# A two-layer convolution block: work moved between ScalarE, VectorE and GpSimd, two transfers reshaped, PSUM banks from a table and a new order of issue

## The chip, the core and the metric

The kernel runs on one core of one Trainium2 chip. A core has TensorE (PE in the profile; its weight loads are listed as PEld), VectorE (DVE), ScalarE (ACT), GpSimd (POOL) and SyncE (SP), each with its own queue of instructions that it works off in order; SP's queue here issues nearly all DMAs. The engines meet at semaphores. SBUF is the on-chip working memory with 128 partitions; PSUM holds eight banks of 128 x 512 floats, into which TensorE writes. The metric is device time in microseconds of the whole launch, lower is better. All data are 32-bit floats.

## What is computed

Input: 16 images of 256 channels, 64 x 64 pixels. Two layers follow one another; the helper names are those of the reference, and what doesn't matter here is cut.

```python
x = x + attention(_gn(x), g_norm, w_qkv, w_out, b_out, g_out)       # layer 0
x = x + experts(_gn(x), router_w, router_b, dw_w, dw_b, pw_w, pw_b)  # layer 1

def attention(x, ...):                    # linear attention, 4 heads of 32
    xn = rmsnorm(x, g_norm)               # over channels, per pixel
    q, k, v = split(einsum('oc,bchw->bohw', w_qkv, xn))
    q = softmax(q, axis=-2); k = softmax(k, axis=-1)
    context = einsum('bhdn,bhen->bhde', k, v)
    out = einsum('bhde,bhdn->bhen', context, q * scale)
    out = einsum('oc,bchw->bohw', w_out, out) + b_out
    return rmsnorm(out, g_out)            # the "output norm"

def experts(x, ...):                      # 2 of 4 experts per image
    w = renormalised top-2 of softmax(mean(x) @ router_w.T + router_b)
    return sum(w[e] * (pw_w[e] @ gelu(depthwise3x3(x, dw_w[e]) + dw_b[e]) + pw_b[e]))
```

`_gn` is a group norm with 32 groups over an image. The experts of an image cannot begin before its router has chosen, and the router needs the mean of the whole image after layer 0.

## The kernel before

A test at the start takes the fast branch, `pipelined_path`; the other branch, `general_path`, does not run here. In the fast branch every step of every image is a small Python function (`norm`, `turn_x`, `out_norm`, `tap1`, ...). A row for each is entered in a list with a phase ("in", "q", "out", "route", "c", "v", "x"), an image number b and a group, quarter or half. A table of numbers, `PLAN` (lines 60 to 819, some 3100 entries), gives each row a place in time; `place` adds the image's start, the group's slot and the step's own entry, or an override for one image and group (`"tap18@e2.3"`: second image from the end, quarter 3). The rows are sorted by place and issued in that order, so the order of each engine's queue is the order of that list. Nothing rearranges it afterwards. An image's period is 64 units of the plan. Three phases of three images overlap: while TensorE and VectorE work on the experts of image b, layer 0 of image b+1 and the statistics of b+2 run between.

Layer 0 works in 8 groups of 512 pixels (`NG`, `GT`). For a group: `load_b` fetches the two halves of 128 channels, `norm` (L1019) applies the group norm; images 0 and 1 (`EARLY`) do it on VectorE, the others on ScalarE, in 224 instructions of 128 x 512. TensorE transposes to pixels (`turn_x`), ScalarE squares and sums, GpSimd makes the reciprocal root (`token_scale`, through `rsqrt`, L956), TensorE projects q and k (`project`), ScalarE takes the exponent (`evacuate`), `context` accumulates. GpSimd divides q by its sums in place (`q_norm`). Once the image's context is mixed with the output weights, `attend` (L1155) makes the output of 256 pixels into a bank `po`; ScalarE squares it (`out_squares`), GpSimd makes the scale s (`out_scale`), and `out_norm` (L1176) multiplies `po` by s into the tile `ob`. In images 0, 1 and 15 ScalarE does that, as two instructions of 128 x 256; in the 13 others VectorE, as one of 128 x 512. `out_turn` (L1185) transposes `ob` back on TensorE, `out_add` (L1193) adds it to the image on VectorE. Reading `po` in `out_norm` is what frees that bank.

The router's chain (`gn1_sums` to `pick_taps`, L1210 to L1283) is a run of small instructions, nearly all of them on VectorE; `expert_index` gives SyncE the number of the expert for `fetch`, and `lace` puts the fetched weights in place on GpSimd.

Layer 1 treats its channels in two ways. The first 128 (functions with a 0) run on TensorE as a banded product: `pad0` writes the padded image into SBUF, `lay` stores it in HBM, `spread` (L1384) reads it back as patches, 54 rows of 1054 floats for each half r of the partitions and each t of eight; four patch buffers `xr` rotate. `conv0` multiplies, `gelu0` evacuates, `put` writes the result to HBM, and `take` (L1454) reads it back by channel into `hp`, 32 rows of 16 KB per transfer. The last 128 (functions with a 1) run as sums on VectorE: `start1` (L1464) opens the sum of an expert on ScalarE with the first tap and the bias, `tap1` (L1472) adds the eight others on VectorE, and `gelu1` follows on ScalarE. `pointwise` (L1484) multiplies both by the experts' weights, and `residual` adds them to the image, from where `store` writes it out.

PSUM: one bank holds the context; the other seven are one rotating pool. `bank` (L971) takes the next of them, so a new tile waits for whoever read the tile seven before it.

Of the kernel before, what the change touches and what calls it, by code (L numbers as in the profile page):

```python
# [24 lines left out]
NE = 4  # L25
# [24 lines left out]
NU = P // (2 * CB)  # L50
NXR = 4
# [9 lines left out]
    "load_x1": 2.02, "mean": 1.19, "means": 13.36, "dev": 13.73, "devs": 17.34, "scale": 17.85,  # L61
    "bias": 21.91, "in_lead": 26.39, "norm0": -8.96, "norm1": -3.87, "turn_x0": 0.72, "x_sq0": 1.77,
    "x_sq1": 2.31, "turn_x1": 1.43, "x_sq2": 3.45, "x_sq3": 3.25, "token": 4.42, "x_keep0": 5.53,
    "x_keep1": 5.77, "x_keep2": 5.97, "x_keep3": 6.03, "project0": 3.18, "evacuate0": 6.05,
    "project1": 3.64, "evacuate1": 6.46, "project2": 3.67, "evacuate2": 6.47, "project3": 4.06,
    "evacuate3": 6.58, "context": 9.48, "q_sum": 8.22, "q_norm": 11.06, "q_turn": 14.73,
    "q_keep": 16.31, "mix_a": 9.53, "mix_turn": 10.09, "mix_v": 11.08, "mix_vv": 11.63,
    "mix_b": 11.82, "mix_out": 13.35, "mix_c": 13.91, "mix_lead": 16.02, "attend0": -1.14,
    "out_sq0": -0.04, "out_sq1": 0.35, "out_scale0": 0.42, "out_norm0": 1.58, "attend1": -0.28,
    "out_sq2": 1.31, "out_sq3": 1.37, "out_scale1": 3.18, "out_norm1": 4.28, "out_turn0": 5.64,  # L70
    "out_add0": 6.51, "sq_sums0": 8.92, "out_turn1": 6.16, "out_add1": 7.06, "sq_sums1": 9.17,
    "sums1": 9.6, "means1": 9.77, "scale1": 10.52, "router": 10.97, "route": 11.89, "choose": 13.68,
    "pick_taps": 21.03, "route_lead": 21.97, "weigh": 29.78, "pick_bias": 41.15, "pad1": -10.35,
    "start0": -0.53, "tap01": 1.33, "tap02": 1.57, "tap03": 1.59, "tap04": 1.87, "tap05": 2.54,
    "tap06": 4.55, "tap07": 4.74, "tap08": 6.14, "gelu10": 13.51, "start1": 1.94, "tap11": 3.52,
    "tap12": 8.13, "tap13": 8.14, "tap14": 8.54, "tap15": 9.95, "tap16": 12.84, "tap17": 13.06,
    "tap18": 14.42, "gelu11": 15.46, "pw00": 16.32, "pw01": 16.45, "pw02": 17.78, "pw03": 17.83,
    "pw10": 16.09, "pw11": 16.24, "pw12": 19.85, "pw13": 20.43, "residual00": 19.8,
    "residual01": 20.37, "store0": 32.19, "residual10": 22.5, "residual11": 23.44, "store1": 26.19,
    "in_first": 0.96, "in_more": 1.71, "q_first": 3.46, "out_first": 27.07, "out_more": 37.75,  # L80
    "q_less": 0.19, "load_a0": -17.62, "load_a1": -6.91, "load_b0": -15.96, "load_b1": -6.67,
    "stats0": -13.55, "stats1": -1.94, "load_weights": 58, "scale_weights": -7.03,
    "end_pw00": 135.48, "end_pw01": -49.35, "end_pw02": 69.96, "end_pw03": 337.87,
    "end_residual00": 3.29, "end_residual01": 66.1, "end_pw10": 115.56, "end_pw11": -47.98,
    "end_pw12": -196, "end_pw13": -114.87, "end_residual10": -13.43, "end_residual11": 88.85,
    "x_0": 0.99, "x_1": -0.21, "x_2": -0.19, "x_e1": 5.09, "x_e2": 4, "route_0": -3.83,
    "route_1": 0.32, "route_2": -0.55, "route_e1": -1.2, "route_e2": -0.21, "out_0": -5.81,
    "out_1": -0.4, "out_2": 0.09, "out_e1": -1.85, "out_e2": -0.87, "q_0": -7.21, "q_1": -2.22,
    "q_2": 0.4, "q_e1": -1.65, "q_e2": -0.57, "in_0": -22.93, "in_1": 7.98, "in_2": 2.65,
    "in_e1": -1.58, "in_e2": 0.28, "pw04": -112.48, "pw14": -23.18, "x_last": 16.71,  # L90
    "v_last": 15.93, "v_e1": 3.4, "tap18@e2.3": 12.73, "start0@e1.3": -0.55, "x_sq2@2.2": 2.88,
    "gelu11@e1.2": 17.06, "tap03@0.1": 1.97, "project0@0.0": 2.01, "out_norm1@2.7": 4.71,
    "out_sq1@e2.0": 0.64, "out_scale1@1.2": 2.19, "evacuate0@1.2": 5.17, "context@1.7": 8.38,
    "out_scale1@0.0": 4.74, "q_norm@0.0": 15.63, "out_turn0@1.4": 5.23, "token@2.1": 4.75,
    "project0@2.7": 3.47, "context@0.7": 8.6, "attend1@e1.3": -2.08, "out_norm1@1.1": 3.87,
    "context@2.1": 7.79, "q_norm@0.6": 12.94, "out_norm0@1.1": 1.4, "gelu11@e2.3": 13.29,
    "evacuate2@1.7": 6.62, "out_norm1@0.6": 4.18, "evacuate2@2.2": 6.81, "project0@2.3": 4.02,
    "token@2.2": 4.19, "norm0@0.0": -14.16, "q_sum@0.0": 10.99, "x_sq2@2.6": 2.62,
    "norm1@0.0": -4.28, "out_norm1@e1.1": 5.78, "x_sq2@1.2": 2.18, "tap04@e2.2": 2.29,
    "x_keep0@0.5": 6.43, "out_turn0@1.2": 5.58, "evacuate3@1.7": 8.13, "x_sq2@2.5": 2.77,  # L100
    "turn_x0@0.0": -3.93, "out_scale0@1.2": 2.15, "tap13@2.0": 6.26, "x_keep3@1.2": 6.99,
    "out_turn0@1.3": 4.82, "q_sum@e2.6": 8.44, "x_sq2@0.0": -1.29, "scale1@0.0": 11.1,
    "token@0.1": 2.33, "q_sum@1.5": 10.67, "q_sum@1.1": 7.71, "tap12@e1.1": 3.08,
    "x_keep1@0.1": 3.76, "evacuate2@1.6": 5.71, "q_sum@1.3": 8.05, "route@0.0": 12.55,
    "x_sq2@1.4": 2.43, "q_turn@0.2": 15.05, "bias@0.7": 26.53, "token@1.4": 3.4,
    "pick_taps@e1.0": 23.22, "out_add0@2.5": 6.36, "means@0.7": 10.61, "dev@e2.7": 6.55,
    "evacuate3@1.2": 6.52, "x_sq3@1.4": 3.12, "x_keep1@0.7": 6.49, "mix_v@0.7": 11.95,
    "token@1.1": 4.49, "tap17@e2.3": 11.87, "out_turn0@e1.1": 7.3, "token@0.2": 4.15,
    "q_sum@1.2": 9.02, "out_norm0@1.2": 4.52, "x_keep0@0.7": 6.45, "mix_b@e1.7": 12.79,
    "choose@1.0": 14.4, "project0@e1.7": 2.76, "tap07@e1.2": 8.15, "tap11@e1.2": 5.96,  # L110
    "means@1.7": 3.31, "token@1.3": 3.93, "q_sum@e1.6": 8.87, "tap12@e2.0": 8.3,
    "out_scale0@1.3": 2.06, "route@e1.0": 12.62, "pick_taps@2.0": 19.25, "out_turn0@1.0": 5.21,
    "scale@0.7": 20.54, "tap06@e1.0": 3.75, "out_turn1@e2.2": 8.74, "token@0.7": 3.73,
    "q_sum@e2.7": 9.96, "stats0@e2.5": -12.47, "out_turn0@1.5": 5.79, "token@1.6": 3.52,
    "q_turn@e2.1": 14.09, "out_norm1@e2.5": 4.67, "weigh@0.0": 26.02, "x_sq2@1.0": 3.24,
    "out_turn0@0.3": 5.99, "turn_x0@2.2": -1.78, "mix_b@0.7": 18.63, "out_scale1@e2.6": 2.5,
    "gelu11@e1.0": 17.52, "token@e2.7": 4.04, "context@1.2": 12.21, "q_sum@e2.0": 7.26,
    "tap01@e1.3": 1.63, "tap12@e2.2": 6.87, "x_sq2@1.6": 3.27, "load_a1@1.6": -5.34,
# [704 lines left out]
def pipelined_path(ctx, tc, ring, st_0, wqkv, x, w_outT, b_out, g_out, router_wT, router_b, dw, dw_b, pwT, pw_b, out):  # L823
# [103 lines left out]
    def band_table():  # L927
# [5 lines left out]
        for dy in range(3):  # L933
            for dx in range(3):
# [5 lines left out]
                for u in range(QR, QR + dy):  # L940
                    k = 3 * QR + 2 * dx + u - QR
                    nc.gpsimd.tensor_copy(te[:, :, k * QR + u - dy : k * QR + u - dy + 1], w)
# [1343 lines left out]
```

## Time and profile before

| | us |
|---|---|
| runs of the kernel, median of 3 | 2681.89 |
| lowest and highest of them | 2674.61, 2682.42 |
| the profiled execution: time | 2665.43 |
| the profiled execution: span, first to last instruction | 2663.7 |
| granted clock of TensorE, mean | 0.97 |

The page of the profile gives for each engine how long it was busy, and cuts the span into 40 equal slices. In the first rows a digit is the busy share of a slice in tenths, in PEclk the clock granted to TensorE in tenths of full speed:

```profile
PE   6897999989899998989999898999989899997877
DVE  6565789879988898989988898988888888889887
ACT  3588988878788888878888887988888788875632
PEclk9998999999999999999999999999999999998999
DMA  4848788878778778777877887787877777866885
```

The middle of the run is even: one image follows another. The first three slices (the first image has nothing to overlap with) and the last four (the last image's experts) look different. A group of instructions is listed with its line, engine, operation, the tiles out<-in, count, busy time and mean; these are the groups that the change touches:

```profile
L1027 ACT ACTIVATE xg<-xb,bi,sc 128x512 f32<-128x512 f32 x224 | 182.6, 815 | 16.9 <-DMA xb<-in_x 14.4 <-PE pq L1066 2.3
L1467 ACT ACTIVATE acc<-pd,ds 128x1024 f32<-128x1024 f32 x128 | 158.9, 1242 | 21.5 <-PE pw L1503 11.7 <-POOL taps L1333 6.4 <-issue 1.7
L1183 DVE TENSOR_TENSOR ob<-po,s 128x512 f32<-128x512 f32 x208 | 141.3, 679 | 35.1 <-POOL s L960 33.6 <-PE tr L1188 1.2 <-POOL s L959 0.2
L1181 ACT ACTIVATE ob<-po,s 128x256 f32<-128x256 f32 x96 | 40.1, 479 | 14.6 <-POOL s L960 14.4
L1474 DVE SCALAR_TENSOR_TENSOR acc<-pd,ds,acc 128x1024 f32<-128x1024 f32 x1024 | 1324.0, 1298 | 44.7 <-ACT acc L1467 26.2 <-DMA xr<-lay 3.1
```

The time behind the second bar is the idle time of the engine just before those instructions, and what ended it.

### The profile page before, as it was taken

What the parts mean: (1) busy time and instruction counts of PE and PEld (TensorE: products, weight loads), DVE (VectorE), ACT (ScalarE), POOL (GpSimd) and SP (SyncE); (2) the same over time, 40 slices, a digit from 0 to 9 for tenths busy, and PEclk for the clock granted to TensorE, in tenths of its full rate; (3) what the DMA queues carried; (4) which work ended last, traced back from release to release, by engine and by line L of the source; (5) the groups of instructions that cost most, each with busy time, mean ns of one, the idle gap of its engine ahead of it and who ended that gap; (6) DMA issues with size and microseconds to landing.
All of it is one profiled execution on the core that took longest, in us unless ns stands there. A gap on an engine that the chain in (4) does not pass through costs nothing.

```text
span 2663.7 us, 50175 instructions
## 1 busy us (share of the span) xinstructions
PE 2404.0 (90%) x17204; PEld 1604.7 (60%) x17204; DVE 2244.2 (84%) x3489; ACT 2072.5 (78%) x4848; POOL 912.5 (34%) x1217
## 2 busy tenths in 40 slices
PE   6897999989899998989999898999989899997877
PEld 5675666656665665656666565666666566564433
DVE  6565789879988898989988898988888888889887
ACT  3588988878788888878888887988888788875632
POOL 4243343333333333334333243432333343433200
PEclk9998999999999999999999999999999999998999
DMA  4848788878778778777877887787877777866885
GB/s 145 103 127 224 227 230 233 232 226 242 221 226 238 227 236 247 228 227 228 232 228 240 240 240 222 230 235 228 247 216 222 222 206 209 232 186 197 227 226 176
DMA packets 410840, 581.15 MB, mean 218 GB/s; under 512 B 66000, under 2 KB 279504, under 8 KB 406480
## 3 DMA queue, kind: packets, MB, share of 16 engines
q1 hardware_dynamic: 377248, 575.36, 74.8%
q10 hardware_dynamic: 33328, 2.49, 1.6%
q8 instruction: 139, 2.28, 0.4%
q14 instruction: 125, 1.02, 0.1%
HBM read 402.49 MB, written 175.24 MB: 217 GB/s over the span
## 4 chain that ended last, share of the span: by engine, by line
PE 43%; DVE 21%; DMA 15%; ACT 8%; issue 6%; POOL 3%; SPq 3%; DVEq 0%; ACTq 0%; POOLq 0%
PE pw L1503 19%; DVE acc L1474 11%; PE pq L1066 7%; DMA hid<-hx 5%; PE pc L1084 4%; PE po L1160 4%; DMA hp<-hid 4%; PE dw L1432 3%; PE px L1035 2%; PE tr L1188 2%; DVE ring L1518 2%; DVE ob L1183 2%; DMA xr<-lay 2%; DVE ring L1197 2%; DMA lay<-pd 2%
## 5 line engine op out<-in xcount | busy, mean ns | idle before, releaser
L1474 DVE SCALAR_TENSOR_TENSOR acc<-pd,ds,acc 128x1024 f32<-128x1024 f32 x1024 | 1324.0, 1298 | 44.7 <-ACT acc L1467 26.2
L1503 PE MATMUL pw<-acc,ps 128*128 128x512 f32 x1024 | 496.5, 623 | 26.8 <-ACT acc L1482 24.4
L1066 PE MATMUL pq<-wqkv_n,xg 128*128 128x256 f32 x2048 | 487.5, 385 | 13.7 <-ACT e L1074 3.5
L1503 PE MATMUL pw<-hp,ps 128*128 128x512 f32 x1024 | 479.9, 604 | 18.4 <-DMA hp<-hid 15.5
L959 POOL TENSOR_SCALAR s<-ss 128x2 f32<-128x2 f32 x256 | 125.5, 490 | 1020.6 <-ACT junk L1168 1015.4
L1066 PEld LDWEIGHTS pq<-wqkv_n,xg 128*128 128x128 f32 x2048 | 383.1, 192 | 90.4 <-issue 19.1
L1503 PEld LDWEIGHTS pw<-acc,ps 128*128 128x128 f32 x1024 | 191.1, 199 | 229.9 <-issue 154.8
L1503 PEld LDWEIGHTS pw<-hp,ps 128*128 128x128 f32 x1024 | 189.2, 193 | 204.7 <-issue 196.5
L1042 ACT ACTIVATE jx<-px 128x256 f32<-128x256 f32 x512 | 196.3, 383 | 131.8 <-PE px L1035 122.4
L1160 PE MATMUL po<-mw,qt 128*128 128x256 f32 x1024 | 265.1, 389 | 9.9 <-DVE ring L1197 3.8
L1518 DVE SCALAR_TENSOR_TENSOR ring<-pw,bs,ring 128x512 f32<-128x512 f32 x248 | 180.8, 744 | 107.5 <-PE pw L1503 104.5
L1074 ACT ACTIVATE e<-pq,r 128x256 f32<-128x256 f32 x512 | 210.8, 477 | 58.8 <-PE pq L1066 45.0
L1197 DVE SCALAR_TENSOR_TENSOR ring<-tr,gout,ring 128x512 f32<-128x512 f32 x256 | 187.1, 746 | 81.2 <-PE tr L1188 75.9
L1084 PE MATMUL pc<-xt,e 128*128 128x257 f32 x1024 | 252.4, 389 | 2.5 <-ACT xt L1053 1.7
L960 POOL TENSOR_TENSOR s<-s,mhalf 128x2 f32<-128x2 f32 x256 | 243.7, 952 | 21.4
L1168 ACT ACTIVATE junk<-po 128x256 f32<-128x256 f32 x512 | 198.0, 387 | 60.9 <-PE po L1160 52.1
L1432 PE MATMUL dw<-xr,taps 55*32 55x128 f32 x8192 | 185.4, 283 | 61.7 <-DMA xr<-lay 30.0
L1188 PE MATMUL tr<-ident,ob 128*128 128x128 f32 x1024 | 162.1, 285 | 67.6 <-DVE ob L1183 46.4
L1160 PEld LDWEIGHTS po<-mw,qt 128*128 128x128 f32 x1024 | 186.0, 194 | 61.5 <-issue 22.0
L1432 PEld LDWEIGHTS dw<-xr,taps 55*32 55x32 f32 x8192 | 128.5, 108 | 147.0 <-issue 28.1
L1444 ACT ACTIVATE hx<-dw 128x512 f32<-128x512 f32 x256 | 148.4, 594 | 86.9 <-PE dw L1432 60.8
L1084 PEld LDWEIGHTS pc<-xt,e 128*128 128x128 f32 x1024 | 191.2, 195 | 33.2 <-issue 5.1
(146 smaller groups left out, 3533.4 us busy)
## 6 DMA issues: line engine op xcount, KB each, us to landing
xr<-lay SPq DMA_DIRECT2D x512, 197.6 KB
hid<-hx SPq DMA_DIRECT2D x256, 256.0 KB
hp<-hid SPq DMA_DIRECT2D x128, 512.0 KB
out<-ring SPq DMA_DIRECT2D x128, 512.0 KB
xa<-in_x SPq DMA_DIRECT2D x240, 256.0 KB
xb<-in_x SPq DMA_DIRECT2D x240, 256.0 KB
ring<-in_x SPq DMA_DIRECT2D x120, 512.0 KB
lay<-pd SPq DMA_DIRECT2D x32, 1188.0 KB
```

The source lines that it names most:

```text
L960: nc.gpsimd.tensor_tensor(out_t, out_t, mhalf[:, :n], ALU.pow)
L1066: nc.tensor.matmul(pq, xg[:, k, c * P : (c + 1) * P], wqkv[:, k, : 2 * HID], start=(k == 0), stop=(k == KH - 1),)
L1074: nc.scalar.activation(live["e", b, g][:, c], live["pq", b, g, c // 2][:, c % 2], AF.Exp, scale=live["r", b, g][:, c : c + 1],)
L1084: nc.tensor.matmul(live["pc", b], live["e", b, g][:, c, HID:], xt[g % 2][:, c], start=(g == 0 and c == 0), stop=(g == NG - 1 and c == CG - 1),
L1160: nc.tensor.matmul(po[:, c], qt[:, n * P : (n + 1) * P], live["mw", b], start=True, stop=True)
L1168: nc.scalar.activation(junk[:, :C], live["po", b, g, hf][:, c], AF.Square, accum_out=ss[:, c : c + 1])
L1188: nc.tensor.transpose(tr[:, c * P : (c + 1) * P], live["ob", b, g, c // 2][:, c % 2, k * P : (k + 1) * P], ident,)
L1197: nc.vector.scalar_tensor_tensor(xin, live.pop(("tr", b, g, k)), gout[:, k : k + 1], xin, ALU.mult, ALU.add, accum_out=live["sm", b][:, 0, ...
L1432: nc.tensor.matmul(pair[r][g * 2 * QR : (g + 1) * 2 * QR, s * HC : (s + 1) * HC], taps[ks, CB * t + i].rearrange("p i x -> p (i x)"), stri ...
L1474: nc.vector.scalar_tensor_tensor(acc, pd1[j % 2][:, t // 3 : t // 3 + QR, t % 3 : t % 3 + W], live["ds", b][:, i, t : t + 1], acc, ALU.mul ...
L1503: nc.tensor.matmul(po, w, rhs, start=begin, stop=end)
L1518: nc.vector.scalar_tensor_tensor(xo, po, bs, xo, ALU.add, ALU.add)
```

## The change

Six edits:

1. `norm` for images 2 to 15 goes from ScalarE to GpSimd, one tensor_scalar of 128 x 512 with two per-partition scalars each.
2. `start1` goes from ScalarE to GpSimd, one tensor_scalar of 128 x 1024 each.
3. `out_norm` of all images is two ScalarE instructions of 128 x 256; the VectorE form is gone.
4. `spread` reads the 54 rows of a half in one transfer instead of 48 and 6; the rows of the patch, and of the band table that it is multiplied with, are numbered 3u + dx throughout.
5. `take` reads 32 rows as four pieces of 4 KB each; the tile `hp` has four floats of padding behind each piece, so that pieces do not join, and `pointwise` indexes it accordingly.
6. `bank` takes a bank's number from a string, `BANKS`, one digit for each call, instead of rotating; `PLAN` has new numbers throughout (3121 entries), which sort the rows into a new order on every queue.

```diff
+HR = QR // 2 * HC
...
+BANKS = (
+    "012345601320463150361423640516352314306203502416502431414205206543125351025364351456320352"
...
+)
...
-        tb = work.tile([P, TOPK * QR * HC], FP, tag="hp", name="bands", bufs=1)
-        tb = tb[:, : NE * KP * QR]
+        tb = work.tile([P, 2 * TOPK, HR + 4], FP, tag="hp", name="bands", bufs=1)
+        tb = tb.rearrange("p s n -> p (s n)")[:, : NE * KP * QR]
...
-                    k = 3 * QR + 2 * dx + u - QR
+                    k = 3 * u + dx
...
+    turns = iter(BANKS)
...
     def bank(*key):
-        return banks.tile([P, 512], FP, tag="bank", name="_".join(map(str, key)))
+        tag = f"bank{next(turns)}"
+        return banks.tile([P, 512], FP, tag=tag, name="_".join(map(str, key)), bufs=1)
...
-            nc.scalar.activation(live["xg", b, g][:, k], xb, AF.Identity, bias=bi, scale=sc)
+            nc.gpsimd.tensor_scalar(live["xg", b, g][:, k], xb, sc, bi, ALU.mult, ALU.add)
...
         ob = new(work, [P, 2, C], "ob", b, g, hf, bufs=3)
         s, po = live.pop(("s", b, g, hf)), live.pop(("po", b, g, hf))
-        if b in (0, 1, NB - 1):
-            for c in range(2):
-                nc.scalar.activation(ob[:, c], po[:, c], AF.Copy, scale=s[:, c : c + 1])
-        else:
-            nc.vector.tensor_tensor(ob, po, s.unsqueeze(2).to_broadcast([P, 2, C]), ALU.mult)
+        for c in range(2):
+            nc.scalar.activation(ob[:, c], po[:, c], AF.Copy, scale=s[:, c : c + 1])
...
-            k0 = r * P // 2
-            (su, _), run1 = run.ap
+            rows, run1 = run.ap
             nc.sync.dma_start(
-                out=tile_t[k0 : k0 + 3 * QR, :n],
-                in_=bass.AP(run.tensor, run.offset, [[su, QR], [1, 3], run1]),
-            )
-            nc.sync.dma_start(
-                out=tile_t[k0 + 3 * QR : k0 + WK, :n],
-                in_=bass.AP(run.tensor, run.offset + QR * su, [[1, 3], [su, 2], run1]),
+                out=tile_t[r * P // 2 : r * P // 2 + WK, :n],
+                in_=bass.AP(run.tensor, run.offset, [rows, [1, 3], run1]),
             )
...
-            new(work, [P, TOPK * QR, HC], "hp", b, h, bufs=1)
+            new(work, [P, 2 * TOPK, HR + 4], "hp", b, h, bufs=1)
...
-            out=live["hp", b, h][cs].rearrange("c k x -> c (k x)"), in_=hids[h][cs]
+            out=live["hp", b, h][cs, :, :HR], in_=hids[h][cs].rearrange("c (s n) -> c s n", n=HR)
...
-        nc.scalar.activation(
-            acc, pd1[j % 2][:, 0:QR, 0:W], AF.Identity,
-            bias=ds[:, i, 9:10], scale=ds[:, i, 0:1],
+        nc.gpsimd.tensor_scalar(
+            acc, pd1[j % 2][:, 0:QR, 0:W], ds[:, i, 0:1], ds[:, i, 9:10], ALU.mult, ALU.add
         )
...
-                rhs = hp[:, i * QR + rows.start : i * QR + rows.stop, j % NB2 * W : (j % NB2 + 1) * W]
+                rhs = hp[:, 2 * i + q, :HR].rearrange("p (r x) -> p r x", x=HC)
+                rhs = rhs[:, :, j % NB2 * W : (j % NB2 + 1) * W]
```

The numbers of `PLAN` are left out. Per image, the new order puts 6 taps, no output norm and 2 statistics on VectorE's queue between the group-norm sums and the end of the tap choice, where 10 taps, 3 output norms and 4 statistics stood before; the count of every kind of instruction is otherwise as the six edits say.

## The prediction

> **What bounds the kernel now.** I read the busy table first, then the chain of waits, the waits of TensorE, a table of windows, and a timeline of one stall. The busy table and the chain:
>
> ```profile
> PE 2404.0 (90%) x17204; PEld 1604.7 (60%) x17204; DVE 2244.2 (84%) x3489; ACT 2072.5 (78%) x4848; POOL 912.5 (34%) x1217
> PE 43%; DVE 21%; DMA 15%; ACT 8%; issue 6%; POOL 3%; SPq 3%; DVEq 0%; ACTq 0%; POOLq 0%
> ```
>
> TensorE leaves 260 us of the span idle, and no engine owns the chain: it changes hands. About 55 idle us lie in the first 240 us, 60 in the last 284 (windows 0 to 240: 184.8 busy; 2380 to 2664: 224.2), so 145 lie between. There each image takes about 157 us (the DVE line that ends the routing, L1317, comes at 991.4, 1149.1, 1306.1), of which TensorE is busy 148, DVE 139, ACT 131, POOL 55. Eight-microsecond windows say where in an image the 9 idle us are:
>
> ```profile
> 1146.00:1154.00 8.00, 7.38 (x42) 5.71 (x41) 7.51 (x21) 6.53 (x17) 3.24 (x6) 1.00 0.65 205
> 1154.00:1162.00 8.00, 3.98 (x18) 3.01 (x18) 7.93 (x12) 7.66 (x20) 4.32 (x5) 0.88 1.10 259
> 1162.00:1170.00 8.00, 7.89 (x18) 4.04 (x19) 6.03 (x13) 6.18 (x10) 2.32 (x3) 0.69 0.91 252
> ```
>
> Columns after the length are PE, PEld, DVE, ACT, POOL busy, then the granted clock. TensorE falls to half, DVE is full, and the clock then drops. The timelines of TensorE, DVE and GpSimd name the cause:
>
> ```profile
> 1157.83 0.41 PE L1188 MATMUL tr<-ident,ob 128*128 128x128 f32 x2 [0.26 <-DVE ob L1183]
> 1162.11 0.69 PE L1188 MATMUL tr<-ident,ob 128*128 128x128 f32 x2 [3.87 <-DVE ob L1183]
> ...
> 1183.89 1.04 PE L1432 MATMUL dw<-xr,taps 55*32 55x128 f32 x30 [2.23 <-DVE ob L1183]
> ```
>
> ```profile
> 1157.61 3.26 DVE L1474 SCALAR_TENSOR_TENSOR acc<-pd,ds,acc 128x1024 f32<-128x1024 f32 x2
> 1160.79 0.68 DVE L984 BATCH_NORM_STATS2 st<-xa 128x6 f32<-128x512 f32 x1
> 1161.39 0.67 DVE L1183 TENSOR_TENSOR ob<-po,s 128x512 f32<-128x512 f32 x1
> ```
>
> ```profile
> 1157.97 1.81 POOL L1099 TENSOR_TENSOR e<-e,qs 128x512 f32<-128x512 f32 x1
> ```
>
> The output norm (L1183) stands on DVE behind two taps (L1474). They take 3.26 us instead of 2.57: GpSimd's product waited for one tap, then the next tap waited for it. The second stall is a bank: the convolution needs one that the norm has yet to read. So this stretch, from the group-norm sums to the first convolution, is DVE's; most of the rest of the image is TensorE's.
>
> ```profile
> PE tr L1188 <- DVE ob L1183: 46.4, 29, 4.1
> PE dw L1432 <- DMA xr<-lay: 30.0, 29, 4.3
> ...
> PE dw L1432 <- DVE ob L1183: 16.0, 8, 2.3
> PE pw L1503 <- DMA hp<-hid: 15.5, 14, 2.1
> PE tr L1188 <- ACT ob L1181: 12.1, 10, 4.2
> ```
>
> **Output norms to ScalarE.** DVE loses 208 x 679 ns = 141 us, ACT gains 416 x 479 ns = 199 us. Of TensorE's idle time, 46.4 + 16.0 = 62 us ended on the DVE norm. What is late next is the ACT norm: images 0, 1 and 15 already have it, and their 48 norms cost 12.1 us of waits, 8.8 of them in the last 284 us where TensorE starves anyway; the 32 others cost 3.3 us, 0.10 each. 208 x 0.10 = 21, so **-41 us** (ends: -10 at 0.25 each, -62 at none). In the new order some 2.2 us of ACT work (median) lie between the second square and its norm; GpSimd's scale needs 0.23 + 0.71 us undisturbed, 1.1 + 1.7 when a tap holds it up. So it is hidden mostly, not always. ACT's program holds as many table loads as before (200 and 198 in the two branches together), so none is added.
>
> **DVE's order.** From the group-norm sums to the end of the tap choice DVE now does 10 taps, 3 norms, 4 statistics; in the new order 6, 0 and 2, all else equal: 4 x 1.284 + 3 x 0.679 + 2 x 0.679 = 8.5 us less per image. TensorE's order in that stretch hardly moves. The two named stalls were 6.1 of it; of the other 2.4 x 14 images = 34 us I take a third, **-12 us**, as the displaced work comes back later, where TensorE is the bound and hides it (ends 0 and -34).
>
> **The clock.** The granted clock was at half for 85 us between 249 and 2416, after such stalls: 42 us of lost work. [...] I take half, **-21 us** (ends 0 and -42).
>
> **Input norms and openings to GpSimd.** ACT loses 224 x 815 + 128 x 1242 ns = 342 us; with the norms gained, its net is -142 us, from 78% to 73%. GpSimd's cost for them is not in the trace. Nearest row, one tensor input: the copy of 128x1024, median 1.04 us undisturbed; upper end the two-input product, 1.05 us for 512. So 128 x 1.04 + 224 x 0.53 = 252 us (upper 509). [...] What reaches DVE: today's 160 long GpSimd operations stretched only 44 taps beyond 1.45 us, by 21 us in all, because most began beside a DVE operation on PSUM. Per new operation I allow between that 0.13 us and its whole length: 40 to 252 us on DVE; I take 90, since openings stand near the taps. DVE has 420 idle us; only the DVE-led stretch, about 34 of 157 us, passes it on: **+20 us** (ends 0 and +252 less the 141 removed). Behind a waiting input norm on GpSimd stand the scales: in the new order 108 of 256 have a norm directly ahead, 17 an opening. That is up to 0.5 or 1.0 us more before an output norm, within the 0.10 above unless the load of xb is late (it made ACT wait 14.4 us over the run).
>
> **Patch and read-back.** SyncE loses 512 issues of 735 ns (L1397), 377 us of queue time; each patch pair now takes two issues instead of four. Before conv 0 of the image shown, the first eight pairs of issues ran from 1160.2 to 1172.8. [...] For the read-back, 16 KB packets took 1112 ns mean, 4096 B ones 193: four cost 772, so 4235 of them save 340 ns each, 90 us per engine of about 2050 busy. TensorE waited 30.0 us for patches and 15.5 for the read-back. I take under half of it off: **-20 us** (ends -45 and +20, if nine engines make patches late).
>
> **Banks.** A table instead of rotation: each tile waits for one named reader. Not shown by the trace; the waits for readers of other tiles are of the size of the L1183 bank wait, already counted. **0** (ends -25, +25).
>
> **Sum:** -41 - 12 - 21 + 20 - 20 = -74 us. The profiled execution took 2665.4; that gives 2591. The median of the timed runs is 16.5 us above it, so **2608 us**.
>
> **Rivals.**
> A. [...] GpSimd's 252 us of one-input work lands on the taps. If all reaches DVE's queue, DVE is busy 2244 - 141 + 252 = 2355, +111 us, and at unchanged waits the time is about 2793; it decides from 141/252 = 56% of the added time reaching DVE, and half of that excess gives about 2735. For it: DVE at 84%, taps are 59% of its busy time. Against: the 21 us measured today, and DVE's own idle time. 14%.
> B. *The wait changes its name.* TensorE waits for the ACT norm as long as for DVE's, because ACT or the scale is late: 0.30 us per norm as before; only patches and order help, DVE delays eat that: 2682, about -10 to +10. For it: the 4.2 us wait for the ACT norm in the tail. 8%.
> C. *TensorE becomes the bound.* All of the 145 us between the ends go: 2404 + 115 = 2519, or 2536 as a median. For it: DVE and ACT both fall, and both stalls per image share one cause. Against: DVE would need 93% or more all along. 15% for the region under 2560.
> [...] 13%, still faster.
> The forecast has 50%. Changes within 0.3%, 8 us, cannot be told from none. Faster 0.78, within 0.06, slower 0.16. The likeliest case alone spans 2570 to 2645; with the others 2535 to 2700.
>
> **What would show it.** Right: no wait of TensorE on DVE's ob; under 25 us on ACT's; images nearer 151 us; the clock above 0.98; DVE between 2150 and 2250 with openings of about 1.1 us on GpSimd; the read-back in 4 KB packets, and the second patch issue gone. Wrong: taps longer than 1.4 us on average, openings of 2 us or more, TensorE waiting for patches much beyond 30 us, or GpSimd's scales ending its long waits.

## The result, and the profile after

The changed kernel took 2643.1 us (median; 2642.0 to 2651.4) against 2678.3 (2672.4 to 2682.4) for the kernel before on the same chip: ratio 0.9878, interval 0.9862 to 0.9893. It is faster, by about 33 us where the sum said 74. The profiled execution took 2643.4. That of the kernel before took 2665.4, less than all four timed runs of it here, so the two profiles show 22 of the 33 us.

The busy table of the changed kernel:

```profile
PE 2385.0 (90%) x17204; PEld 1599.1 (61%) x17204; DVE 2196.4 (83%) x3281; ACT 1919.2 (73%) x4910; POOL 1452.7 (55%) x1569
```

TensorE is busy 2385 of 2641.6 us, so 257 us are idle, where it was 260 before. The idle time stayed; the busy time of the same 17204 matmuls fell by 19 us, and why is not shown in full. The clock, taken up below, can be a part of it: in the kernel before, the pointwise products took a median of 592 ns from 1450.3 to 1455, at a granted clock of 1.00, and 1061 ns from 2474.3 to 2481.1, at 0.50. The waits of TensorE (engine, tile and line; waited for; us, times, longest):

```profile
PE pw L1523 <- DVE ring L1222: 36.2, 10, 5.1
PE pw L1523 <- DMA hp<-hid: 32.8, 16, 4.9
PE dw L1452 <- DMA xr<-lay: 20.4, 18, 7.4
PE tr L1213 <- ACT ob L1208: 15.3, 7, 9.1
PE pw L1523 <- ACT acc L1501: 13.6, 12, 2.5
```

The wait on VectorE's norm is gone, and the wait on ScalarE's norm is small: 15.3 us. But two others have grown: 36.2 us for VectorE's residual add `out_add` (L1222; 1.6 before), and 32.8 us for the read-back (15.5 before). The timeline of one image shows where the first stands, TensorE first, then VectorE, then ScalarE (start, us, instruction, idle before and its releaser):

```profile
1155.97 1.03 PE L1188 MATMUL po<-mw,qt 128*128 128x256 f32 x4
1161.37 9.84 PE L1523 MATMUL pw<-acc,ps 128*128 128x512 f32 x16 [4.37 <-DVE ring L1222]
```

```profile
1156.01 3.95 DVE L1493 SCALAR_TENSOR_TENSOR acc<-pd,ds,acc 128x1024 f32<-128x1024 f32 x3
1159.87 0.69 DVE L1012 BATCH_NORM_STATS2 st<-xa 128x6 f32<-128x512 f32 x1
1160.48 0.73 DVE L1222 SCALAR_TENSOR_TENSOR ring<-tr,gout,ring 128x512 f32<-128x512 f32 x1
```

```profile
1159.99 1.06 ACT L1501 ACTIVATE acc<-acc 128x1024 f32<-128x1024 f32 x1 [0.57 <-DVE acc L1493]
```

TensorE stops at the same place as before the change, for 4.4 us, and the pointwise product of the last quarter now takes the place of the transposes. It needs a PSUM bank that `out_add` has yet to read, behind three taps on VectorE. The GELU of those taps, which the same product reads, ends at 1161.05, only 0.3 us before the product starts. From the routing line (L1342) of one image to that of the next, about 154 us pass in the middle of the run (about 157.5 before); the forecast's own sign was 151.

### The profile page after: what moved, and what is told of

It is laid out like the page before. It is cut to its first block, busy times and chain, and to the rows that moved or that the text cites. A ratio compares the mean times of both kernels' runs of the same rounds, so it can differ in the third digit from the quotient of the medians.

```text
span 2641.6 us, 49408 instructions
## 1 busy us (share of the span) xinstructions
PE 2385.0 (90%) x17204; PEld 1599.1 (61%) x17204; DVE 2196.4 (83%) x3281; ACT 1919.2 (73%) x4910; POOL 1452.7 (55%) x1569
## 2 busy tenths in 40 slices
DMA packets 418002, 581.07 MB, mean 220 GB/s; under 512 B 60880, under 2 KB 274384, under 8 KB 417744
## 4 chain that ended last, share of the span: by engine, by line
PE 45%; DMA 17%; DVE 13%; POOL 10%; ACT 9%; issue 5%; SPq 2%; DVEq 0%; ACTq 0%; POOLq 0%
PE pw L1523 20%; PE pq L1094 8%; DMA hid<-hx 6%; DVE acc L1493 6%; DMA hp<-hid 4%; PE pc L1112 4%; PE dw L1452 4%; PE po L1188 3%; PE px L1063 2%; DMA xr<-lay 2%; POOL s L986 2%; PE tr L1213 2%; POOL acc L1487 2%; POOL xg L1055 2%; DVE st L1012 1%
## 5 line engine op out<-in xcount | busy, mean ns | idle before, releaser
L1493 DVE SCALAR_TENSOR_TENSOR acc<-pd,ds,acc 128x1024 f32<-128x1024 f32 x1024 | 1391.1, 1365 | 39.9 <-POOL acc L1487 25.8
L1523 PE MATMUL pw<-acc,ps 128*128 128x512 f32 x1024 | 486.3, 621 | 56.4 <-DVE ring L1222 36.2
L1523 PE MATMUL pw<-hp,ps 128*128 128x512 f32 x1024 | 486.9, 612 | 50.7 <-DMA hp<-hid 32.8
L1055 POOL TENSOR_SCALAR xg<-xb,sc,bi 128x512 f32<-128x512 f32 x224 | 268.9, 1201 | 147.6 <-PE pq L1094 125.6
L1487 POOL TENSOR_SCALAR acc<-pd,ds 128x1024 f32<-128x1024 f32 x128 | 198.5, 1551 | 274.5 <-PE pw L1523 248.8
L985 POOL TENSOR_SCALAR s<-ss 128x2 f32<-128x2 f32 x256 | 152.7, 597 | 275.2 <-ACT junk L1196 263.6
L1208 ACT ACTIVATE ob<-po,s 128x256 f32<-128x256 f32 x512 | 214.2, 476 | 114.9 <-POOL s L986 113.9
L1070 ACT ACTIVATE jx<-px 128x256 f32<-128x256 f32 x512 | 198.5, 388 | 131.2 <-PE px L1063 121.6
L986 POOL TENSOR_TENSOR s<-s,mhalf 128x2 f32<-128x2 f32 x256 | 273.1, 1067 | 21.3
L1081 ACT ACTIVATE xt<-px,r 128x256 f32<-128x256 f32 x448 | 180.6, 477 | 94.3 <-POOL r L986 92.9
L1112 PE MATMUL pc<-xt,e 128*128 128x257 f32 x1024 | 247.0, 384 | 0.6 <-DVE xt L1079 0.6
L1222 DVE SCALAR_TENSOR_TENSOR ring<-tr,gout,ring 128x512 f32<-128x512 f32 x256 | 183.6, 743 | 74.2 <-PE tr L1213 68.1
L1188 PEld LDWEIGHTS po<-mw,qt 128*128 128x128 f32 x1024 | 183.3, 193 | 61.6 <-issue 14.3
```

What stands on the lines that cost most here:

```text
L986: nc.gpsimd.tensor_tensor(out_t, out_t, mhalf[:, :n], ALU.pow)
L1055: nc.gpsimd.tensor_scalar(live["xg", b, g][:, k], xb, sc, bi, ALU.mult, ALU.add)
L1070: nc.scalar.activation(junk[:, :C], live["px", b, g, c // 2][:, c % 2], AF.Square, accum_out=ss[:, c : c + 1])
L1112: nc.tensor.matmul(live["pc", b], live["e", b, g][:, c, HID:], xt[g % 2][:, c], start=(g == 0 and c == 0), stop=(g == NG - 1 and c == CG - 1),
L1188: nc.tensor.matmul(po[:, c], qt[:, n * P : (n + 1) * P], live["mw", b], start=True, stop=True)
L1208: nc.scalar.activation(ob[:, c], po[:, c], AF.Copy, scale=s[:, c : c + 1])
```

## The experiments

Each ratio is to the kernel before on the same chip, with its 95% interval; 1% is some 27 us. The changed kernel's 0.9878 is the mark for what is undone in it. It was measured once and not again beside the experiments, so a difference from it carries both intervals, 5 to 9 us in all.

### Is it the bank, or VectorE's queue?

Theory T1: VectorE's queue ahead of the last quarter's product is late, taps as much as adds. Theory T2: the new table put the product on a bank that is held too long.

**Banks in rotation.**

```diff
-        tag = f"bank{next(turns)}"
-        return banks.tile([P, 512], FP, tag=tag, ..., bufs=1)
+        return banks.tile([P, 512], FP, tag="bank", ...)
```

> The changed kernel with its banks taken in rotation again (one ring of seven) instead of from the table. The changed kernel measured 2643 us; TensorE waits 36 us for VectorE's out_add, which releases the bank of the last quarter's pointwise product. Theory T1 (VectorE's queue ahead of that product is late: three taps, whose GELU the same product reads, end only 1.2 us before the two adds that release the banks, so another bank brings nothing): the table is worth little, 2640 to 2665, and the wait at the last quarter's product stays at 25 us or more under whatever name. Theory T2 (the table put the product on a bank that is held too long): the wait goes, 2605 to 2630.

0.9957 [0.9938, 0.9976]: the table is worth about 0.8% in this order, and the wait for `out_add` stays (33.6 us). Against T2.

**The adds first.** In images 3 to 11 VectorE's order goes from taps, statistics, adds to statistics, adds, taps; the GELU moves with its taps.

> The changed kernel with the two adds of the second group (and one statistics operation) put ahead of the last three taps of the last quarter on VectorE, in images 3 to 11; no other engine's order changes. T2 (the bank is what the product waits for): the banks are free 4 us earlier in each of 9 images, so about -36 x 9/10, 2605 to 2620. T1 (the taps are as late as the adds): the taps end about 1.4 us later, the product's second operand comes 1.4 us later, TensorE waits for ACT acc instead of DVE ring, 2640 to 2658.

0.9968 [0.9956, 0.9980], slower than either theory said. VectorE's timeline shows a wait that I had put ahead of the adds unseen:

```profile
1157.23 0.69 DVE L1012 BATCH_NORM_STATS2 st<-xa 128x6 f32<-128x512 f32 x1 [3.04 <-DMA xa<-in_x]
1157.84 0.73 DVE L1222 SCALAR_TENSOR_TENSOR ring<-tr,gout,ring 128x512 f32<-128x512 f32 x1
```

The statistics operation waited 3.0 us for its load, and the adds behind it. So this run doesn't decide; the next leaves that operation where it was.

**The adds alone first.** The order is adds, taps, statistics.

> As the run with the adds first, but with the statistics operation left behind the taps, since in that run it waited 3.0 us for its load and held the adds up; images 3 to 11. The adds now follow their transposes at once, and the banks of the last quarter's product are free some 5 us earlier. T2 (the bank is what the product waits for): ratio to the kernel before 0.973 to 0.979 (the changed kernel has 0.9878). T1 (the last three taps and their GELU are as late as the adds): the product's first pair starts early and the second pair waits for ACT acc; nothing gained, 0.986 to 0.992.

0.9944 [0.9923, 0.9965]. The wait for `out_add` has gone from the list; in its place:

```profile
PE pw L1523 <- ACT acc L1501: 49.2, 27, 3.9
```

49.2 us where it was 13.6: the product now waits for the GELU of the taps that were put back. T2 falls; freeing the bank alone gains nothing, and the run is a little slower than T1 said.

**Three taps fewer, in the last quarter, and in the second.** The sum of the second expert lacks three taps in images 3 to 12.

```diff
-                for t in range(1, 9):
+                for t in range(1, 6 if 3 <= b < 13 and (j, i) == (3, 1) else 9):
```

> The changed kernel with three of VectorE's taps left out of the second expert's sum in the last quarter of images 3 to 12 (the sum is short of them): 30 taps of 1024, 39 us of VectorE's 2196. T1 (VectorE's queue ahead of the last quarter's product is the bound there): taps, GELU and adds all come 4 us earlier per image, nearly the whole of it in the time, -30 to -38, ratio 0.973 to 0.977. Rival T4 (the transfers or TensorE decide and the wait at the product only takes up slack): -0 to -12, ratio 0.983 to 0.988.

> The same three taps left out of the second quarter instead of the last (images 3 to 12, 39 us of VectorE). If VectorE bounds the whole image, as much is gained as in the last quarter, -30 to -38 (0.973 to 0.977). T1 as I hold it (VectorE leads only in the stretch ahead of the last quarter's product; in the second quarter TensorE has its own work): -0 to -12, ratio 0.983 to 0.988.

0.9898 [0.9869, 0.9928] and 0.9904 [0.9879, 0.9929]. VectorE does 39 us less in either run and nothing is gained; both points lie above the range of 0.983 to 0.988 (T4 in the first run, T1 in the second), their intervals reach into it. The 0.973 to 0.977 of T1 in the last quarter is excluded: T1 falls too. In the first, the wait for `out_add` fell from 36.2 to 23.4 us, while those for the GELU (13.6 to 18.3) and the read-back (32.8 to 35.7) rose. Shortening a named wait of 36 us was worth nothing that can be told.

**Work in the wait.** The adds first, and the eight products that read `hp` ahead of the eight that read `acc`:

```diff
+        keys = [(b, 3, f"pw{k}") for k in ("12", "13", "02", "03")]
+        ahead = [row for key in keys for row in rows if row[1:4] == key]
...
+        n = [row[1:4] for row in rows].index((b, 3, "pw10"))
+        rows[n:n] = ahead
```

> The adds first as above, and TensorE's eight products of the last quarter that read the read-back hidden rows put ahead of the eight that read the taps' sums, images 3 to 11. If T1 is right, banks alone bring nothing and TensorE can be given 3.6 us of work, which stands behind the wait now, to do in it: about -3.0 x 9 = -27, ratio 0.975 to 0.981. If T2 is right, the adds first have taken the wait away already and this changes nothing against that run. If the transfers decide, 0.986 to 0.990.

1.0161 [1.0135, 1.0186], a clear miss.

```profile
PE pw L1523 <- ACT xt L1081: 56.1, 16, 6.9
```

The products that I moved forward now wait 56.1 us on `x_keep` (L1081), which waits for GpSimd's token scale. As I read it, `x_keep` reads the bank that they are to write: the gap had no free bank to offer.

### The engine moves, undone in the new order

Theory T3: what the moves cost or save is ScalarE's room.

**Input norms of images 3 to 12 back on ScalarE.**

```diff
+            if 3 <= b < 13:
+                nc.scalar.activation(live["xg", b, g][:, k], xb, AF.Identity, bias=bi, scale=sc)
+                return
             nc.gpsimd.tensor_scalar(live["xg", b, g][:, k], xb, sc, bi, ALU.mult, ALU.add)
```

> The changed kernel with the input norms of images 3 to 12 (160 of 208 in all behind the first images) on ScalarE again. My forecast charged norms and openings on GpSimd together 20 us, 6 to 7 us of it the norms. [...] Rival T3 (ScalarE needs the room more than VectorE suffers): 160 x 0.7 us more on ScalarE, its output norm is late again, 2650 to 2680.

0.9903 [0.9888, 0.9918]: undoing costs 0.25%, about 7 us, at the near edge of T3's range and at the limit of what can be told. The taps fell to a mean of 1339 ns (1365 in the changed kernel, 1298 before), and the waits of `x_keep` for GpSimd's token scale from 92.9 to 68.7 us. So the norms on GpSimd do lengthen VectorE's taps, and that does not set the time.

**Openings of images 3 to 12 back on ScalarE** (`start1`, in the same form).

> The changed kernel with the openings of the experts' sums of images 3 to 12 (80 of 128) on ScalarE again. T1: VectorE's taps are slowed by the openings on GpSimd (the opening holds GpSimd 1.2 to 1.6 us); taps 1365 ns to about 1335, 2625 to 2643. Rival T3 (ScalarE's room decides): 80 x 1.1 us more on ScalarE, 2650 to 2690.

0.9871 [0.9856, 0.9886]: no difference that can be told, with the taps at 1348 ns. For the openings T3 isn't borne out.

**Output norms of images 2 to 14 back on VectorE** (what was expected draws on runs that are told further down).

```diff
-        for c in range(2):
-            nc.scalar.activation(ob[:, c], po[:, c], AF.Copy, scale=s[:, c : c + 1])
+        if b in (0, 1, NB - 1):
+            ...
+        else:
+            nc.vector.tensor_tensor(ob, po, s.unsqueeze(2).to_broadcast([P, 2, C]), ALU.mult)
```

> The changed kernel with the output norms of images 2 to 14 on VectorE again, all else as changed. My forecast's -41 for this move, undone: 1.000 to 1.006. As the norms alone (they made the kernel before slower, 1.0049): no loss, 0.983 to 0.990. If the new order is fitted to norms on ScalarE (order with moves undone gave 1.0153): 1.000 to 1.015, whatever the norms are worth themselves.

1.0450 [1.0427, 1.0474], three times what I had expected at most: the new order cannot bear the norms on VectorE. VectorE now waits 131.2 us ahead of the norms, for GpSimd's scale:

```profile
DVE ob L1211 <- POOL s L986: 131.2, 54, 4.6
```

In the kernel before that wait was 33.6 us. In the changed kernel ScalarE waits for the same scale, and TensorE's transposes wait only 15.3 us behind it:

```profile
ACT ob L1208 <- POOL s L986: 113.9, 76, 6.3
```

As I read it, the new order puts each norm so close behind its squares that the engine which has it stands still until the scale is there; ScalarE can spare that time, and VectorE, with the taps in the same queue, cannot.

### The pieces in the old order

With VectorE and the banks out, two theories were left. T4: the transfers decide. T5: the order is fitted to the pieces, and the pieces alone are worth little.

**One edit to the kernel before: output norms of images 3 to 12 on ScalarE too.**

```diff
-        if b in (0, 1, NB - 1):
+        if b in (0, 1, NB - 1) or 3 <= b < 13:
```

> The kernel before with one edit: the output norms of images 3 to 12 on ScalarE as well (160 of 208 that were VectorE's). My forecast: 62 us of TensorE's waits go, 21 return, -41 for 208, so -31 for 160, less what ScalarE's load adds since here it still has the input norms and openings: ratio 0.988 to 0.995. T4/T5 (the wait changes its name): 0.997 to 1.008.

1.0049 [1.0035, 1.0064]: slower. Its waits of TensorE:

```profile
PE tr L1188 <- ACT ob L1181: 57.8, 29, 4.2
PE dw L1432 <- DMA xr<-lay: 46.1, 41, 4.5
```

The transposes wait 57.8 us, 29 times, for ScalarE, where they waited 46.4 us, 29 times, for VectorE. The wait has changed its name.

**The old order and rotating banks with all other edits** (output norms of images 2, 13 and 14 left on VectorE).

> The kernel before's order of issue and its rotating banks with all other edits (output norms on ScalarE in all images but 2, 13 and 14; input norms and openings on GpSimd; patches in one transfer; 4 KB read-back). T5 (the new order and table are what makes the moved work pay): as slow as before or slower, ratio 0.998 to 1.015. If the pieces carry the gain, 0.985 to 0.992.

1.0014 [0.9996, 1.0032]. All pieces together gain nothing in the old order.

```profile
PE tr L1212 <- ACT ob L1205: 54.1, 28, 3.6
PE dw L1451 <- DMA xr<-lay: 32.3, 31, 4.2
```

ScalarE has lost input norms and openings here (1245 us busy from 400 to 2000, by the windows view; 1424 in the run above), yet the transposes wait nearly as long and as often. So it isn't ScalarE's load. Nor is it GpSimd's, which makes the scale: 908 us in the same stretch, and 966 in the changed kernel, where the wait is 15.3 us. Nor the banks: with the banks in rotation and the new order (the first experiment) the wait is 14.3 us. What is left, images 2, 13 and 14 apart, is the order, and ScalarE's queue shows what about it. First TensorE and ScalarE in this run:

```profile
1175.07 0.84 PE L1212 MATMUL tr<-ident,ob 128*128 128x128 f32 x2 [3.64 <-ACT ob L1205]
```

```profile
1170.21 0.83 ACT L1205 ACTIVATE ob<-po,s 128x256 f32<-128x256 f32 x2
...
1171.93 1.28 ACT L1500 ACT_TABLE_LOAD   x1
1173.23 1.06 ACT L1500 ACTIVATE acc<-acc 128x1024 f32<-128x1024 f32 x1
...
1174.55 0.83 ACT L1205 ACTIVATE ob<-po,s 128x256 f32<-128x256 f32 x2
```

Then ScalarE at the same place of the changed kernel:

```profile
1152.46 0.83 ACT L1208 ACTIVATE ob<-po,s 128x256 f32<-128x256 f32 x2
...
1154.47 0.84 ACT L1208 ACTIVATE ob<-po,s 128x256 f32<-128x256 f32 x2
...
1155.70 1.28 ACT L1501 ACT_TABLE_LOAD   x1
1156.99 1.06 ACT L1501 ACTIVATE acc<-acc 128x1024 f32<-128x1024 f32 x1
```

In the old order a GELU, with the load of its table, stands between the two norms of this group and holds the second back: it starts 4.3 us behind the first, and TensorE waits 3.6. In the new order the GELU comes behind both, and the second norm starts 2.0 us behind the first. Either order is the same in the second and the sixth group of each of the images 5 to 12, where these waits lie (1.4 us in the sixth). The plan's numbers say the same: the old order issues the transpose of a group 1.36 units of its plan behind the second norm ("out_norm1" 4.28, "out_turn0" 5.64), the new one 3.06 ("out_norm1" 2.64, "out_turn0" 5.7).

### The transfers

**Patch in two transfers again.**

```diff
...
-                out=tile_t[r * P // 2 : r * P // 2 + WK, :n],
-                in_=bass.AP(run.tensor, run.offset, [rows, [1, 3], run1]),
+                out=tile_t[k0 : k0 + 3 * QR, :n],
+                in_=bass.AP(run.tensor, run.offset, [[su, QR], [1, 3], run1]),
+            )
+            nc.sync.dma_start(
+                out=tile_t[k0 + 3 * QR : k0 + WK, :n],
+                in_=bass.AP(run.tensor, run.offset + QR * su, [[1, 3], [su, 2], run1]),
```

> The changed kernel with each patch in two transfers again (48 rows and 6 rows, and the table's rows in the order that belongs to them). Taking three taps an image off VectorE moved the time by under 0.3%, in either quarter, so VectorE's queue is not the bound (T1 falls), and banks that come free earlier brought nothing (T2 falls). T4 (transfers decide: as soon as one wait is shortened the waits on the read-back grow, 33 us to 36-44 us): the second issue and the fuller engines cost 10 to 25 us, ratio 0.991 to 0.997. T5 (the order of issue is fitted to the pieces, and the pieces alone are worth little): the same direction, under 8 us, 0.987 to 0.991.

1.0077 [1.0064, 1.0090]: this one part is worth 2.0% in the new order, 53 us, more than twice the most that T4 expected. The wait that grows is not the patches':

```profile
PE pw L1528 <- DMA hp<-hid: 48.9, 21, 6.4
...
PE dw L1457 <- DMA xr<-lay: 9.1, 11, 4.4
```

The read-back is waited for 48.9 us (32.8), the patches 9.1 (20.4). Both are issued by SyncE, one behind the other.

**The patch in one transfer alone, in the kernel before.** Theory T6: this transfer is the gain itself, whatever the order.

> The kernel before with one edit: each patch in one transfer of 54 rows instead of 48 and 6. T5 (the order decides: all pieces in the old order gave 1.0014, the norms alone 1.0049): the patch alone gives little, ratio 0.994 to 1.000. T6 (the patch's transfer is the gain itself, whatever the order): 0.978 to 0.988.

0.9897 [0.9868, 0.9927], some 27 us: nearly the whole of what the full change brings. The point lies between the two ranges; its interval reaches into T6's and not into T5's. Of TensorE's waits, those on the read-back fell from 15.5 us to 5.0, while those on the patches themselves rose from 30.0 to 39.1:

```profile
PE dw L1427 <- DMA xr<-lay: 39.1, 40, 5.0
...
PE pw L1498 <- DMA hp<-hid: 5.0, 4, 1.7
```

**Read-back in 16 KB packets again** (`hp` unpadded, the transfer as it was).

> The changed kernel with the read-back in 16 KB packets again. My forecast counted the 4 KB packets as part of a gain of 20 us. T4 with the patches as the carrier: undoing it costs 5 to 20 us, ratio 0.990 to 0.996. Rival: the read-back got worse with the change (TensorE's waits on it rose from 15.5 to 32.8 us), undoing it gains 5 to 17 us, 0.981 to 0.986.

0.9856 [0.9836, 0.9876]: the 4 KB form gains nothing. The point lies in the rival's range; the 6 us that the form would cost are within the noise. The lines of its issue, in the changed kernel and in this one (ns: least, median, most):

```profile
L1480 SPq DMA_DIRECT2D hp<-hid x128: 538/578/2047, 243.7 to 2605.4; - x128
```

```profile
L1480 SPq DMA_DIRECT2D hp<-hid x128: 302/334/2273, 243.7 to 2595.8; - x128
```

An issue of the 4 KB form takes SyncE 578 ns instead of 334.

**Is it the second issue (T7) or the spread over DMA engines (T8)?** First, 48 rows of each patch only: one issue, with the transfer of the first piece of the version in two. The last 6 rows are not loaded, so the first depthwise part lacks their data.

> The changed kernel with the first 48 rows of each patch only: the last 6 are not loaded, so the first depthwise part misses those taps' data. One issue a patch, as in the changed kernel, and 11% fewer bytes. T7 (the second issue in the queue is what cost 2%): 0.983 to 0.989, as the changed kernel. T8 (the spread over the engines is what costs): the 48 rows go over the engines as in the version in two, 0.997 to 1.005.

0.9793 [0.9769, 0.9817]: faster than the changed kernel and than T7 said, as bytes and issue time both fall; T8 falls. No run shows on which DMA engines a transfer's packets run; the pages count 64465 packets under 512 B here, 66000 with the patch in two and 60880 in the changed kernel, so the 48 rows took 7 small packets more for each of 512 patches than the 54 did, and were faster. Then the changed kernel with an issue added that moves nothing to speak of:

```diff
+            spare = small.tile([1, 1], FP, tag="spare", name=..., bufs=8)
+            nc.sync.dma_start(out=spare, in_=b_out[:, 0:1])
```

> The changed kernel with a second, nearly empty transfer behind every patch (4 bytes into a spare tile that nothing reads): 512 more issues in SyncE's queue, no more data to speak of. T7 (the issue is what the second piece costs): most of the 2% comes back, 0.997 to 1.008. If the data and the engines of the second piece are what cost: 0.986 to 0.991.

1.0033 [1.0018, 1.0048]: 1.55%, 41 us, for 512 transfers of 4 bytes. T7 holds, and it is again the read-back that is waited for longer (54.5 us; 32.8 in the changed kernel), not the patches:

```profile
PE pw L1525 <- DMA hp<-hid: 54.5, 22, 5.3
...
PE dw L1454 <- DMA xr<-lay: 19.8, 20, 7.3
```

No run separates the issue of these small transfers from their completion. The issue lines, first of the changed kernel, then of the kernel with the patch in two, then of this one:

```profile
L1417 SPq DMA_DIRECT2D xr<-lay x512: 731/752/2311, 207.9 to 2591.8; - x171
```

```profile
L1418 SPq DMA_DIRECT2D xr<-lay x512: 557/569/1726, 208.0 to 2627.4; - x171
```

```profile
L1422 SPq DMA_DIRECT2D xr<-lay x512: 706/717/1262, 208.7 to 2628.0; - x171
```

```profile
L1422 SPq DMA_DIRECT2D spare<-in_b_out x512: 225/414/1067, 209.9 to 2630.6; - x171
```

From such medians I get the queue time that each run adds to SyncE; beside it stand the same from the sum of all of SyncE's issues in the traces, and what the time did (difference of ratios times 2668 us; ±5 to ±8 us each):

| against the changed kernel | SyncE's issue time, from medians | all issues summed | time |
|---|---|---|---|
| patch in two | 512 x (569 + 717 - 752) ns = +273 us | +301 | +53 us |
| empty issue | 512 x (414 + 767 - 752) = +220 | +231 | +41 |
| 48 rows (fewer bytes too) | 512 x (549 - 752) = -104 | -71 | -23 |
| read-back in 16 KB | 128 x (334 - 578) = -31 | -40 | -6 |

The first two lie near 0.2 us of time for 1 us in the queue. The 48 rows gain more for their queue time, but move fewer bytes as well, and the last row can't be told from nothing. In the old order, the patch alone took 512 x (753 - 579 - 717) = -278 us out (-292 summed), and 27 us off: 0.1.

### Order and patch, and the best version

**The new order, table and one-transfer patch, the rest undone** (engine moves in images 3 to 12, read-back in all).

> The changed kernel's order, table and one-transfer patch, with the other moves undone in images 3 to 12: input norms and openings on ScalarE, output norms on VectorE; and the read-back in 16 KB packets in all images. If order and patch are the whole gain: 0.984 to 0.992. If the order needs the moved work to pay (norms on the engine that it was made for): 0.995 to 1.015.

1.0153 [1.0130, 1.0176], at the upper edge of what was expected: the order needs the work where it was laid out for. VectorE waits 122.4 us for the scale ahead of its norms here.

**Openings of images 3 to 12 on ScalarE and read-back in 16 KB, all else as changed.**

> The changed kernel with the two moves undone that a run showed to bring nothing: openings of images 3 to 12 on ScalarE, read-back in 16 KB packets. Alone they gave 0.9871 and 0.9856 beside the changed kernel's 0.9878. If both gains add: 0.982 to 0.986. If each lies within what the measurement can tell: 0.986 to 0.989.

0.9835 [0.9812, 0.9858]: the fastest that leaves no work out, some 0.4% below the changed kernel, with intervals that just do not meet. That is in the range for gains that add, though the interval reaches to the edge of the other.

## Why the forecast was right in direction and wrong in size

The old-order runs split the result into the forecast's own steps. Each is a difference of ratios, ±4 to ±8 us; the third is what is left over, ±10. The split holds for this path alone: the new order and table with the patch, but without the engine moves, were slower than the kernel before (1.0153), so the steps do not simply add.

| step | forecast | measured |
|---|---|---|
| output norms to ScalarE | -41 | +13 alone (160 of 208) |
| patch (with read-back) | -20 | -27 alone (patch) |
| input norms and openings (and read-back in the last column) | +20 | +18, as 1.0014 less the two above |
| VectorE's order, clock, banks | -12, -21, 0 | -36, from 1.0014 to 0.9878 |
| sum | -74 | -33 |

**The failed step is the output norms, "so -41 us".** The forecast read 62 us of waits that ended on VectorE's norm, took them as gone and let 21 come back, at 0.10 us for each norm as in images 0, 1 and 15. Alone, the move left the transposes' wait at 57.8 us under ScalarE's name, and at 54.1 with ScalarE relieved. The cover "hidden mostly" was read from the new order and credited to the engine. It is the order that hides the chain of squares, scale and norm, by keeping the GELU behind both norms. Rival B, "the wait changes its name", was the right description of the move alone, at 8%. In the new order the move can't be priced alone: its undoing costs 5.7%, with VectorE waiting 131 us for the scale, and 2.8% when the other moves are undone too (in ten images instead of thirteen).

**The sign that the forecast asked for came true and didn't carry the time.** No wait on VectorE's `ob`, 15.3 us on ScalarE's (under 25 asked), yet TensorE's idle time stayed at 257 us. Other waits ended at almost the same point of the image, on `out_add`, the GELU and the read-back. The runs at that point show that shortening one by itself gains nothing. So the 62 us of named waits were replaced and not saved.

**Patch and read-back: mechanism right, size wrong.** The forecast gave SyncE's 377 us less queue time and took 20 off. The term was mis-sized in both factors: the one issue that stays grows from 579 to 752 ns and each read-back issue from 353 to 578, so the queue lost 278 - 29 = 249 us by medians, 295 when all issues are summed; and each us of it was worth 0.1 in the old order and 0.2 in the new. It looked for the worth in the waits on patches (30 us) and on 4 KB packets, which brought nothing. What the shorter queue relieved were the waits on the read-back, which stands in the same queue: 15.5 to 5.0 us in the old order, and 48.9 to 32.8 in the new. No run shows the nine engines behind the end of +20: the traces don't say on how many DMA engines a patch runs. What they show is that packets under 512 B fell from 66000 to 60880 in both orders, 10 for each of 512 patches, and that in both TensorE waits longer for the patches themselves when they come in one transfer (39.1 us against 30.0 in the old, 20.4 against 9.1 in the new); that is below the gain, and its cause is open.

**GpSimd: +20 was of the right size in the old order, as far as a remainder of +18 ±10 can tell; in the new one it costs nothing that can be told.** The norms took 1201 ns and the openings 1551 in the mean where 530 and 1040 were said, and the taps went from 1298 to 1365 ns: 1024 x 67 ns = 69 us on VectorE, beside the 90 allowed. But undoing the norms costs 7 us and undoing the openings nothing, and 39 us of VectorE's taps were worth nothing. Rival A was right that the taps would grow, and wrong on the price. The forecast's reason for the 44 stretched taps, that most of the 160 long GpSimd operations began beside a VectorE operation on PSUM, isn't in the trace of the kernel before: 29 of them did, with a median of 1048 ns; 47 began with VectorE idle (1044 ns) and 51 beside a tap (1622 ns).

**Order and clock.** The two terms, -33, stand against -36 measured for order and table together. That they meet does not show that they were right for their reasons. Banks were put at 0 with ends of ±25; rotation costs 21 us in this order, so the table is part of it. On the clock the two profiled executions say little: the mean granted clock went from 0.970 to 0.972, and the work that was withheld (one minus the clock, times the span) from 80 to 74 us. But the kernel before had a mean clock of 0.9655 in its 74 timed runs beside the experiments, the old order with all edits 0.966 in its 12, the changed kernel 0.972 in its four: 92, 90 and 73 us withheld. So up to 19 us may be the clock's, of the 21 forecast, though 0.98 was not reached. No run changes the clock by itself, so this part is not shown as a cause. The half that the forecast took of its 42 us was the author's estimate; no run shows which of an image's stalls has to go for a drop to go. In windows of 1 us of the kernel before (columns as in the forecast) the clock falls at 1160, some 2 us into the gap of 3.87 us, which begins at 1158.2:

```profile
1159.00:1160.00 1.00, 0.00 (x0) 0.00 (x0) 1.00 (x1) 0.99 (x2) 0.78 (x1) 1.00 1.16 195
1160.00:1161.00 1.00, 0.00 (x0) 0.00 (x0) 1.00 (x2) 0.97 (x5) 0.00 (x0) 0.57 0.82 254
```

In the changed kernel the stall that remains still has its drop (0.52 from 1160 to 1161), and the second drop, at 1184 before, behind a gap of 2.23 us, is gone (1.00 from 1180 to 1187).

What stays open: why a microsecond in SyncE's queue is worth twice as much in the new order. The waits on the read-back suggest an answer (15.5 us before the change and 32.8 after it, so less slack lies ahead of it); no run separates that.

## What to carry to other kernels

A wait in a profile names the last of several arrivals at a point: before counting it as gain, take the named one away and ask what arrives next, in the order that will run. Count every issue on a queue that serves several streams by its duration times its number, for what stands behind it and not only for the transfer itself. Where an order has been fitted to a placement of work, price order and placement together; either alone can be a loss.

## What the runs showed of the hardware

- The time in which SyncE issued a transfer went with its shape and not with its bytes: medians of 549 to 579 ns for 48 rows of a patch, 717 for 6 rows, 752 to 767 for 54, 414 for 4 bytes; for the 512 KB of a read-back, 334 to 353 in 16 KB rows and 578 in padded pieces of 4 KB.
- With the input norms and openings on GpSimd, VectorE's taps took longer: in the old order their mean was 1298 ns without norms and openings there and 1369 with them; in the new order 1365 with all, 1339 with the norms of ten images taken back, 1348 with the openings of ten.
